# A four-layer block on one core: the last two of 39 expert blocks behind a condition, and regrouped activation tables

## The chip, the cores and the metric

The kernel runs on one core of a Trainium2 chip. Its five engines work side by side, each through its own instructions in order, and wait for one another by semaphores: TensorE (PE in the profile, with its weight loads as PEld), VectorE (DVE), ScalarE (ACT), GpSimd (POOL), and SyncE (SP), which here mostly issues transfers. The metric is the time of one execution on the device in microseconds (us); the median of several runs is compared. Everything is computed in 32-bit floats.

## The reference

x is 4 batches of 512 tokens with 512 channels. Four sublayers are added to it in turn. Each takes as input a gated value, a bidirectional decaying scan over the side input f, multiplied by a sigmoid of x:

```python
x = x + mamba2(gate0(x, f))        # 16 heads, inner width 1024, state 128
x = x + experts(gate1(x, f))       # 8 experts, each token goes to its best 2
x = x + attention(gate2(x, f))     # 16 causal heads of 128, keys in 4 groups
x = x + ffn(gate3(x, f))           # inner width 1408, silu(g) * u
```

The Mamba layer ends with a normalization and a projection, in which a weight per channel stands between the two:

```python
yg = yg * rsqrt(mean(yg * yg) + eps)
y = (yg * norm_w) @ out_proj_w.T
```

The expert layer:

```python
top_vals, top_idx = top_k(x @ gate_w.T + gate_b, 2)
routing = softmax(top_vals)
for e in range(8):
    h = x @ w1[e].T + b1[e]
    y = h[:, 0::2] * sigmoid(1.702 * h[:, 0::2]) * (h[:, 1::2] + 1)
    out += (y @ w2[e].T + b2[e]) * sum(routing * (top_idx == e))
```

## The kernel before, in words

Channels lie on the 128 partitions, tokens along the free axis. The program is written as one long unrolled stream, and a scheduler puts each engine's instructions in an order; `after(...)` pins what is written inside it behind the last instruction so far of the named engines.

**Gates.** `gate_pair` computes the part of a gate that doesn't depend on x, for two channel chunks at a time: scans on DVE, Exp and Ln on ACT. `make_gates` is a generator over the pairs; `pump` moves it on by one larger step, `nudge` by a small one. They are called between other work. `gated` loads such a gate, takes Tanh of x on ACT (`apply_gate`, L379 to L385) and multiplies on DVE.

**Activation tables.** ACT computes a function only with the table that holds it. `Tables` (`act`, L96 to L130) lets the kernel place the loads: `act.use(name)` puts one behind all activations that used the last, and `act(...)` an activation behind it. After `act.leave()` (L1400) tables are loaded wherever the compiler finds that one is missing. `LOG_EXP` holds Ln and Exp, `EXP` holds Exp and Tanh.

**Mamba stage** (L861 to L1412). Rows are the four batches, tiles are 128 tokens. The loop at L1298 interleaves, for each tile, the outputs of this tile (`decays`, `outputs`), the end of the tile before it (`squares`, `norm`, `turn`, `project`, `scale`, `add_x`), the start of the next, gate steps, and the routing of the batch before (`choose_experts`, with `logits` and `route`, a generator that is moved on by `next(routing)`). `turn` transposes y on PE and writes it times `norm_w` to yT: the first half by one DVE instruction (L1219), the second by four of ACT (L1227). `sums` forms cumulative sums by products with triangular matrices (L981); it copies the first, cs, out of PSUM (L991), transposes it on PE (L993), and copies that out again for a store (L995). `route` builds one-hot matrices ov and os on DVE (L571 to L574) and multiplies them on PE (L576).

**Expert stage.** Rows are gathered by expert into blocks of 128. However the tokens fall, 4096 rows fill at most 39 blocks (`NBLK`), since each of the 8 experts can leave one partly full. All 39 are computed; a block without tokens gathers a dummy row and its result goes nowhere. The first 17 (`NEARLY`) need only batches 0 to 2 and start within the Mamba stage. `order_blocks` gives each used block its place; of the last 22, those with tokens of batch 0 come first. `Experts.round` (L828) does, for block i: gather block i+3 (POOL), load weights if the expert in this slot changes (SP, a conditional transfer), the first half of the products (pg, pn), the transposes of block i-1, the last product of block i-2 (po), whose result POOL scatters to `rows_o`. Two rounds past the last block drain the pipeline.

The driver (L1476 to L1505) runs the rounds with one `pump` each until round 35, and from round 35 on adds batch 0's results to x (`load_results` by POOL, `add_results`: ACT, DVE, transposes pcb on PE, DVE). Then `early_h`, the first attention input, is gated from x[0], and two more rounds follow, beside which it can be computed.

**Attention** (L1509 to L1671). 64 heads: `queries` of the next head (pq), `scores` of this one (psc, mask and row maximum on DVE, Exp on ACT at L1592, division on DVE), `context` of the last (transposes ptp, copies pT, products pctx), and `dense` after each four. After each softmax row block a `nudge` moves the gates of layers 2 and 3. In the first group, at the second head of batch b, `combine(b + 1)` and the gate of batch b + 1 are written (L1656 to L1658). The feed-forward layer follows with its own loads.

Of the kernel before, what the change touches and what calls it, by code (L numbers as in the profile page):

```python
# [10 lines left out]
F32 = mybir.dt.float32  # L11
# [25 lines left out]
NROW = B * T * TOPK + 1  # L37

NEARLY = -(-((B - 1) * T * TOPK - E * (P - 1)) // P)

FIRST = (T * TOPK + E * (P - 1)) // P

# [38 lines left out]
def block_kernel(ctx: ExitStack, tc: tile.TileContext, a: dict, out: bass.AP):  # L81
# [363 lines left out]


    places = tmp.tile([P, NBLK], I32, tag="th", name="places")
    for lo, hi in ((0, FIRST), (FIRST, NBLK - NEARLY)):
        half = (hi - lo + 1) // 2
        nc.gpsimd.iota(places[:, lo : lo + 2 * half], pattern=[[1, half], [half, 2]], base=lo,  # L450
                       channel_multiplier=0)
# [55 lines left out]
    def route(lg, b, fine):  # L507
        n = NT * E
        bt_ = slice(b * NT, (b + 1) * NT)
        i1, i2, v1, v2 = is1[:, bt_], is2[:, bt_], g1[:, bt_], g2[:, bt_]  # L510
# [52 lines left out]
            nc.vector.tensor_copy(s_, ri)  # L563
            vq.append((q, s_))
        yield
        pt = ps_tp("ptok")
        over = lambda v: v.unsqueeze(2).to_broadcast([P, NT, P])
        lanes = lane.unsqueeze(1).to_broadcast([P, NT, P])
        for c, (q, s_) in enumerate(vq):
            ov = tmp.tile([P, NT, P], F32, tag="th", name="ov")  # L570
            nc.vector.tensor_tensor(ov, lanes, over(q), ALU.is_equal)  # L571
            nc.vector.tensor_tensor(ov, ov, over(res_id[c][:, bt_]), ALU.mult)
            os_ = tmp.tile([P, NT, P], F32, tag="th", name="os")
            nc.vector.tensor_tensor(os_, lanes, over(s_), ALU.is_equal)  # L574
            for t in range(NT):
                nc.tensor.matmul(  # L576
                    pt[:, :P], lhsT=ov[:, t, :], rhs=os_[:, t, :],
                    start=(t == 0 and c == 0), stop=(t == NT - 1 and c == 1),
                )
# [15 lines left out]
    def choose_experts(b, xb, parts, pool, fine=False, **kw):  # L595

        lg = rt.tile([P, NT, E], F32, tag="lg", name="lg", bufs=2)
        nt = NT // parts
        for i in range(parts):
            h = gated(1, b, xb, pool, slice(i * nt * P, (i + 1) * nt * P), **kw)  # L600
            if fine:
                yield
            logits(h, b, lg, i * nt, nt)
            yield
        yield from route(lg, b, fine)
# [6 lines left out]
    eb = rt.tile([1, NBLK], I32, name="eb")  # L612

    def order_blocks(lo, hi):

# [12 lines left out]
        if lo == 0:  # L628
            nc.tensor.matmul(pi[:, P : P + 1], lhsT=tri_lt, rhs=use, start=True, stop=True)
            nc.vector.tensor_copy(rank, pi[:, P : P + 1])  # L630
        else:

            two = rt.tile([P, 2], F32, tag="two", name="two")
            nc.vector.tensor_tensor(jk, sel, cnt[:, NT, :], ALU.mult)
            nc.vector.tensor_reduce(rank, jk, AX.X, ALU.add)
            nc.vector.tensor_scalar(two[:, 0:1], v_lo, rank, use, ALU.is_lt, ALU.mult)
            nc.vector.tensor_tensor(two[:, 1:2], use, two[:, 0:1], ALU.subtract)
            nc.tensor.matmul(pi[:, P : P + 2], lhsT=tri_lt, rhs=two, start=True, stop=True)
            nc.tensor.matmul(pi[:, P + 2 : P + 3], lhsT=ones, rhs=two[:, 0:1], start=True, stop=True)

            nc.vector.tensor_scalar(
                rank, pi[:, P + 1 : P + 2], pi[:, P + 2 : P + 3], two[:, 1:2], ALU.add, ALU.mult
            )
            nc.vector.scalar_tensor_tensor(
                rank, pi[:, P : P + 1], two[:, 0:1], rank, ALU.mult, ALU.add
            )
# [26 lines left out]
    class Experts:  # L673
# [48 lines left out]
        def know(self, n):  # L722

            self.known = n
            for i in range(self.i, min(n, self.i + self.LOOK)):
                self.fetch(i)
            if n == NBLK:
                self.weights(NEARLY)

        def fetch(self, i):  # L730
            if i >= self.known or i in self.hb:
# [96 lines left out]
        def round(self):  # L828
            i = self.i
            self.fetch(i + self.LOOK)  # L830
            if i < NBLK:
# [11 lines left out]
            if i >= 2:  # L843
                self.down(i - 2)
            self.second_weights(i - 2)
            if i < NBLK:
# [14 lines left out]
    with ExitStack() as ph:  # L861
# [63 lines left out]
            nc.sync.dma_start(out=wzt[:, k, :], in_=a["in_projT"][k * P : (k + 1) * P, :DI])  # L925
        nc.sync.dma_start(out=wot, in_=a["out_projT"].rearrange("(k p) m -> p k m", p=P))

        def time_steps(w):

            h = w.h  # L930
# [42 lines left out]
        def sums(w):  # L973
# [13 lines left out]
            dte = sm.tile([P, NT, NH], F32, tag="dte", name="dte", bufs=2)  # L987
            nc.vector.tensor_tensor(dte, dt, ex[:, 1], ALU.mult)

            cs = sm.tile([P, n], F32, tag="cs", name="cs", bufs=2)  # L990
            nc.vector.tensor_copy(cs, pp[:, :n])  # L991
            pcs = ps_tp("pcs")
            nc.tensor.transpose(pcs[:n, :P], cs, ident)  # L993
            csT = four[:n, 0:2, :].rearrange("p i t -> p (i t)")
            nc.vector.tensor_copy(csT, pcs[:n, :P])  # L995
            nc.sync.dma_start(out=cs_d[w.b], in_=csT)
            w.cs, w.ex, w.dte = cs, ex, dte

# [211 lines left out]
        def turn(u):  # L1210

            u.yT = sm.tile([P, NDI, P], F32, tag="yT", name="yT")
            for hh in range(2):
                pyt = ps_tp("pyt")
                for j in range(4):
                    js = slice(j * P, (j + 1) * P)
                    nc.tensor.transpose(pyt[:, js], u.y[hh][:, js], ident)
                if hh == 0:
                    nc.vector.tensor_tensor(  # L1219
                        u.yT[:, :4, :],  # L1220
                        pyt.rearrange("p (j t) -> p j t", t=P),
                        col("norm_w", 0, 4).unsqueeze(2).to_broadcast([P, 4, P]),
                        ALU.mult,
                    )
                else:
                    for j in range(4):
                        nc.scalar.mul(  # L1227
                            u.yT[:, 4 + j, :], pyt[:, j * P : (j + 1) * P], col("norm_w", 4 + j)
                        )

        def project(u):

# [65 lines left out]
        for b in range(B):  # L1298
# [6 lines left out]
            for t in range(NT):  # L1305
# [85 lines left out]
                pump(1, last_gates)  # L1391
                with after(*ENGINES):
                    next(routing, None)
                    if b == B - 1 and t == 1:
# [76 lines left out]
    with tc.tile_pool(name="moe_w2", bufs=1, reuse_waits="tile") as wm:  # L1471
# [4 lines left out]
        def more(limit):  # L1476
            while moe.i < min(limit, moe.known):
                moe.round()
                if moe.i < NBLK - NT:
                    with after(nc.vector):  # L1480
                        pump()

        more(moe.i + 1)
        next(routing)
# [26 lines left out]
    with att as ph:  # L1511
# [64 lines left out]
        def scores(u, i, qT):  # L1576

            prs = []
            for qi in range(NT):
# [12 lines left out]
                nc.scalar.activation(pr, psc[:, :n], AF.Exp, bias=nmax, accum_out=rsum)  # L1592
# [51 lines left out]
        def begin(n):  # L1644
# [4 lines left out]
                groups[g, b] = start_group(g, b, weights[g])  # L1649
            return groups[g, b], queries(groups[g, b], i)  # L1650

        groups = {}
        ready, held = begin(0), None
        for n, (g, b, i) in enumerate(heads_):
            u, qT = ready
            if g == 0 and i == 1 and b + 1 < B:  # L1656
                combine(b + 1)
                hs[b + 1] = gated(2, b + 1, x[b + 1], gp, tag="h", name=f"h2_{b + 1}")  # L1658
            if n + 1 < len(heads_):
                ready = begin(n + 1)  # L1660
            prs = scores(u, i, qT)
            if held is not None:
                old, done = held
# [5 lines left out]
        dense(held[0])  # L1669
        for _ in making:  # L1670
            pass  # L1671


    with ExitStack() as ph:
# [9 lines left out]
        for b in range(B):  # L1684
            h = gated(3, b, x[b], gp, tag="h", name=f"h3_{b}")
            hd = []
            for i in range(NFF):
# [12 lines left out]
                nc.scalar.activation(hi, pg, AF.Silu, scale=col("gate_s", i))  # L1700
# [86 lines left out]
```

## Time and profile before

| | |
|---|---|
| median of 3 runs | 2587.08 us (2586.99 to 2592.27) |
| the profiled execution's own time | 2591.44 us |
| its span, first to last instruction | 2589.7 us |
| mean granted TensorE clock | 0.978 |
| PE busy | 2446.0 us |
| DVE busy | 1409.8 us |
| ACT busy | 1032.3 us |
| POOL busy | 250.4 us |
| moved by DMA | 244.09 MB |
| activation table loads | 68, of 1283 ns each |

The profile is one execution; its span and what lies around it make up its time, and it need not be the median run. "Busy" is the time in which an engine had an instruction under way; an idle stretch is put down to what released the next instruction. A matrix product of 128x128 by 128x512 in 32-bit floats appears as two MATMUL instructions. PE is nearly always busy, so a microsecond counts where PE stands still or where PE has less to do.

### The profile page before, as it was taken

The page shows a single profiled execution, that of the slowest core. Times are in us where ns is not written, and L with a number is a line of the kernel's source. Part 1 is how long each engine was busy: PE and PEld are TensorE (multiplying, and loading weights), DVE is VectorE, ACT ScalarE, POOL GpSimd, SP SyncE. Part 2 cuts the span into 40 slices and gives each one's busy share as a digit, 9 for nine tenths or more (in the row PEclk, how much of TensorE's full clock was granted, in tenths as well). Part 3 has the DMA queues.
Part 4 walks back from the last instruction along what each step waited for, and adds up shares of the span by engine and source line. Part 5 has one row for each costly group of instructions (what it writes and reads, how often), then busy time and mean ns, then how long its engine had stood idle before and what let it go on. Part 6 is the DMA issues. An engine that isn't in the chain of part 4 may idle for free.

```text
span 2589.7 us, 24584 instructions
## 1 busy us (share of the span) xinstructions
PE 2446.0 (94%) x8204; PEld 1301.0 (50%) x8204; DVE 1409.8 (54%) x2786; ACT 1032.3 (40%) x2129; POOL 250.4 (10%) x301
## 2 busy tenths in 40 slices
PE   3889998999999999999989999999999999999999
PEld 1555555556544444445545555555555554444444
DVE  8789998997335555646686554556544441010010
ACT  4666756657222333325554444344443431000000
POOL 1031323313211111120000000000000000000000
PEclk9979998999899999999999999999999999999999
DMA  6222523324244697745231101110000012000000
GB/s 217 77 94 76 188 69 112 131 80 159 66 175 140 223 337 283 274 177 163 75 92 46 46 27 29 45 45 30 21 25 17 17 69 82 17 0 16 8 8 16
DMA packets 88510, 244.09 MB, mean 94 GB/s; under 512 B 9536, under 2 KB 19136, under 8 KB 79296
## 3 DMA queue, kind: packets, MB, share of 16 engines
q1 hardware_dynamic: 79200, 215.78, 24.3%
q0 software_dynamic: 6880, 22.55, 2.5%
q10 hardware_dynamic: 2304, 4.20, 0.4%
q8 instruction: 65, 1.06, 0.2%
q14 instruction: 61, 0.50, 0.1%
HBM read 284.82 MB, written 47.05 MB: 128 GB/s over the span
## 4 chain that ended last, share of the span: by engine, by line
PE 75%; DVE 16%; ACT 4%; DMA 3%; issue 1%; POOL 0%; SPq 0%; ACTq 0%; DVEq 0%
PE pd L1629 8%; PE pq L1565 7%; PE pfu L1696 6%; PE pfo L1706 6%; PE pfg L1691 6%; PE pctx L1614 5%; PE po L808 5%; PE pg L775 5%; PE pn L786 5%; PE psc L1582 3%; PE pc L1007 2%; PE po L1235 2%; PE pv L1551 2%; PE ptp L1605 2%; PE pz L1078 2%; PE pk L1543 2%
## 5 line engine op out<-in xcount | busy, mean ns | idle before, releaser
L1565 PE MATMUL pq<-h,wq 128*128 128x512 f32 x512 | 248.0, 600 | 10.9 <-ACT pr L1592 10.9
L1629 PE MATMUL pd<-cx,wd 128*128 128x512 f32 x512 | 222.9, 593 | 1.3 <-DVE xr L1637 1.3
L1007 PE MATMUL pc<-h,wxb 128*128 128x512 f32 x320 | 151.6, 629 | 46.1 <-DVE h L1275 39.0
L1700 ACT ACTIVATE hd<-pfg,cols 128x512 f32<-128x512 f32 x44 | 30.3, 688 | 380.8 <-PE pfg L1691 380.8
L1701 DVE SCALAR_TENSOR_TENSOR hd<-pfu,cols,hd 128x512 f32<-128x512 f32 x44 | 33.0, 751 | 269.1 <-PE pfu L1696 269.0
L1585 DVE TENSOR_TENSOR psc<-psc,mask 128x128 f32<-128x128 f32 x256 | 72.2, 288 | 192.9 <-PE psc L1582 192.9
L1592 ACT ACTIVATE pr<-psc,nmax 128x128 f32<-128x128 f32 (+3 forms) x256 | 135.5, 530 | 95.6 <-DVE nmax L1587 94.9
L1614 PE MATMUL pctx<-pT,v 128*128 128x512 f32 (+3 forms) x512 | 153.6, 443 | 8.5 <-ACT pT L1608 5.1
L1696 PE MATMUL pfu<-h,ffu 128*128 128x512 f32 x352 | 158.7, 592 | 0.8 <-DMA ffu<-in_upT 0.8
L1691 PE MATMUL pfg<-h,ffg 128*128 128x512 f32 x352 | 158.6, 592 | 0.0
L1582 PE MATMUL psc<-kT,qT 128*128 128x128 f32 (+3 forms) x512 | 153.1, 439 | 3.1 <-ACT qT L1573 1.6
L1629 PEld LDWEIGHTS pd<-cx,wd 128*128 128x128 f32 x512 | 95.9, 190 | 116.8 <-issue 110.0
L1706 PE MATMUL pfo<-hd,ffd 128*128 128x512 f32 x352 | 151.7, 592 | 0.0
L775 PE MATMUL pg<-w,hT 128*128 128x512 f32 x312 | 144.7, 606 | 4.3 <-DMA w<-in_w1x 4.3
L1614 PEld LDWEIGHTS pctx<-pT,v 128*128 128x128 f32 x512 | 93.4, 190 | 99.6 <-issue 35.9
L808 PE MATMUL po<-w,yT 128*128 128x512 f32 x312 | 142.3, 596 | 1.2 <-DMA w<-in_w2x 1.2
L786 PE MATMUL pn<-w,hT 128*128 128x512 f32 x312 | 140.7, 592 | 0.0
L1637 DVE TENSOR_TENSOR xr<-xr,pd 128x512 f32<-128x512 f32 x64 | 44.0, 687 | 169.3 <-PE pd L1629 169.3
L1587 DVE TENSOR_REDUCE nmax<-psc 128x1 f32<-128x128 f32 (+3 forms) x256 | 124.0, 486 | 2.6
L1007 PEld LDWEIGHTS pc<-h,wxb 128*128 128x128 f32 x320 | 62.6, 201 | 119.6 <-issue 73.8
L1565 PEld LDWEIGHTS pq<-h,wq 128*128 128x128 f32 x512 | 87.1, 192 | 69.4 <-issue 56.1
L1605 PEld LDWEIGHTS ptp<-ident,pr 128*128 128x128 f32 x640 | 77.8, 142 | 87.4 <-issue 38.4
(308 smaller groups left out, 4220.2 us busy)
## 6 DMA issues: line engine op xcount, KB each, us to landing
w<-in_w1x SPq DMA_DIRECT2D x80, 1024.0 KB
w<-in_w2x SPq DMA_DIRECT2D x40, 1024.0 KB
wb<-in_b1x SPq DMA_DIRECT2D x40, 512.0 KB
lm<-cs SPq DMA_DIRECT2D x32, 512.0 KB
kt<-in_fT SPq DMA_DIRECT2D x62, 256.0 KB
ek<-ek SPq DMA_DIRECT2D x62, 256.0 KB
ekv<-ekv SPq DMA_DIRECT2D x62, 256.0 KB
g<-num SPq DMA_DIRECT2D x30, 512.0 KB
```

What stands on the lines that cost most here:

```text
L775: nc.tensor.matmul(pg, lhsT=hT[:, k, :], rhs=self.w1[s][0][:, k, :], start=(k == 0), stop=(k == NC - 1))
L786: nc.tensor.matmul(pn, lhsT=hT[:, k, :], rhs=self.w1[s][1][:, k, :], start=(k == 0), stop=(k == NC - 1))
L808: nc.tensor.matmul(po, lhsT=yT[:, j, :], rhs=self.w2[s][:, j, :], start=(j == 0), stop=(j == NI - 1))
L1007: nc.tensor.matmul(pc, lhsT=wxb[:, k, m * P : (m + 1) * P], rhs=h[:, k, :], start=(k == 0), stop=(k == NC - 1),)
L1565: nc.tensor.matmul(pq, lhsT=u.wq[:, k, i * KVC : (i + 1) * KVC], rhs=u.h[:, k, :], start=(k == 0), stop=(k == NC - 1),)
L1582: nc.tensor.matmul(psc[:, :n], lhsT=qT[:, qi * P : n], rhs=u.kT[:, :n], start=True, stop=True)
L1592: nc.scalar.activation(pr, psc[:, :n], AF.Exp, bias=nmax, accum_out=rsum)
L1614: nc.tensor.matmul(pctx[:, kj * P :], lhsT=u.v[:, kj, :], rhs=pT[:, kj, kj * P :], start=(kj == 0), stop=(kj == NT - 1),)
L1629: nc.tensor.matmul(po, lhsT=u.wd[:, i, m * P : (m + 1) * P], rhs=u.ctxT[i], start=(i == 0), stop=(i == HPG - 1),)
L1691: nc.tensor.matmul(pg, lhsT=wg[:, k, cs], rhs=h[:, k, :], start=(k == 0), stop=(k == NC - 1))
L1696: nc.tensor.matmul(pu, lhsT=wu[:, k, cs], rhs=h[:, k, :], start=(k == 0), stop=(k == NC - 1))
L1706: nc.tensor.matmul(po, lhsT=wdn[:, i, m * P : (m + 1) * P], rhs=hd[i], start=(i == 0), stop=(i == NFF - 1),)
```

## The change

The number of blocks that are always computed becomes 37 (`ALWAYS`). `order_blocks` also counts the blocks in use behind the first 17 by a product with ones; all engines load that number into a register, and four rounds that compute the last two blocks stand in a part that is entered only if it is over 20. The drain of the first 37 takes the rounds in which the results of batch 0 are added, and `early_h` is written straight before the condition. Rounds in this stretch pump one gate step and two in turn.

```diff
+ALWAYS = NBLK - 2
...
-    for lo, hi in ((0, FIRST), (FIRST, NBLK - NEARLY)):
+    for lo, hi in ((0, FIRST), (FIRST, ALWAYS - NEARLY), (ALWAYS - NEARLY, NBLK - NEARLY)):
...
+            nc.tensor.matmul(pi[0:1, P + 3 : P + 4], lhsT=ones[:, 0:1], rhs=use, start=True, stop=True)
+            nc.vector.tensor_copy(in_use, pi[0:1, P + 3 : P + 4])
...
-                if moe.i < NBLK - NT:
+                if moe.i < ALWAYS - NT + 1:
                     with after(nc.vector):
-                        pump()
+                        pump(1 + moe.i % 2)
...
-        moe.know(NBLK)
+        moe.know(ALWAYS)
         more(NBLK - 8)
...
-        more(min(NEARLY + FIRST + 2, NBLK - NT - 1))
+        more(NEARLY + FIRST + 2)
...
         for t in range(NT):
-            more(moe.i + 1)
+            moe.round()
             with after(nc.tensor, nc.vector, nc.scalar):
                 add_results(0, t, results.pop(t))
...
-        assert moe.i == NBLK
+        assert moe.i == ALWAYS + 2
         early_h = gated(2, 0, x[0], wa, tag="wq", name="h2_0")
-        moe.round()
-        moe.round()
+        used = nc.values_load(in_use[0:1, 0:1], min_val=0, max_val=NBLK)
+        with tc.If(used > ALWAYS - NEARLY):
+            moe.i = ALWAYS
+            moe.know(NBLK)
+            for _ in range(4):
+                moe.round()
```

`Experts.round` and `know` are adapted to the two numbers. With it come changes elsewhere. In attention the softmax's Exp goes through `act` with the LOG_EXP table, the gate of the next batch moves one head later, between two table loads, and the feed-forward's silu goes through `act` too:

```diff
-                nc.scalar.activation(pr, psc[:, :n], AF.Exp, bias=nmax, accum_out=rsum)
+                act(pr, psc[:, :n], AF.Exp, bias=nmax, accum_out=rsum)
...
+        with after(nc.scalar):
+            act.use(act.LOG_EXP)
...
                 combine(b + 1)
-                hs[b + 1] = gated(2, b + 1, x[b + 1], gp, tag="h", name=f"h2_{b + 1}")
             if n + 1 < len(heads_):
                 ready = begin(n + 1)
+            if g == 0 and i == 2 and b + 1 < B:
+                act.use(act.EXP)
+                hs[b + 1] = gated(2, b + 1, x[b + 1], gp, tag="h", name=f"h2_{b + 1}")
+                act.use(act.LOG_EXP)
```

In the Mamba stage `norm_w` is multiplied once into the projection's weights, by POOL, so that `turn` only copies; the transposed cumulative sum is a product of its own; and `route` builds the first pair of one-hot matrices one step earlier, in h1's buffer:

```diff
+        for k in range(NDI):
+            nc.gpsimd.tensor_scalar(wot[:, k, :], wot[:, k, :], col("norm_w", k), None, ALU.mult)
...
+            nc.tensor.matmul(
+                pp[:n, 3 * n : 3 * n + P], lhsT=dA.rearrange("p t h -> p (t h)"), rhs=tri_le,
+                start=True, stop=True,
+            )
             cs = sm.tile([P, n], F32, tag="cs", name="cs", bufs=2)
             nc.vector.tensor_copy(cs, pp[:, :n])
-            pcs = ps_tp("pcs")
-            nc.tensor.transpose(pcs[:n, :P], cs, ident)
             csT = four[:n, 0:2, :].rearrange("p i t -> p (i t)")
-            nc.vector.tensor_copy(csT, pcs[:n, :P])
+            nc.vector.tensor_copy(csT, pp[:n, 3 * n : 3 * n + P])
...
-                if hh == 0:
-                    nc.vector.tensor_tensor(
-                        u.yT[:, :4, :],
-                        pyt.rearrange("p (j t) -> p j t", t=P),
-                        col("norm_w", 0, 4).unsqueeze(2).to_broadcast([P, 4, P]),
-                        ALU.mult,
-                    )
-                else:
-                    for j in range(4):
-                        nc.scalar.mul(
-                            u.yT[:, 4 + j, :], pyt[:, j * P : (j + 1) * P], col("norm_w", 4 + j)
-                        )
+                nc.scalar.copy(
+                    u.yT[:, hh * 4 : (hh + 1) * 4, :].rearrange("p j t -> p (j t)"), pyt
+                )
...
+            if fine and c == 0:
+                both = pool.tile([P, 2, NT, P], F32, **kw)
+                ov, os_ = both[:, 0], both[:, 1]
...
+            if fine and c == 0:
+                yield
```

For the last row one more `next(routing)` makes up for the added step.

More of the change, by code (lines that the diff above doesn't have):

```diff
@@ L505, in logits, with route @@
             nc.sync.dma_start(out=rows_h[lo : lo + P, :], in_=hr)
-    def route(lg, b, fine):
+    def route(lg, b, fine, pool, **kw):
         n = NT * E
@@ L565, in route @@
         yield
-        pt = ps_tp("ptok")
         over = lambda v: v.unsqueeze(2).to_broadcast([P, NT, P])
         lanes = lane.unsqueeze(1).to_broadcast([P, NT, P])
+        pt = None
         for c, (q, s_) in enumerate(vq):
-            ov = tmp.tile([P, NT, P], F32, tag="th", name="ov")
+            if fine and c == 0:
+                both = pool.tile([P, 2, NT, P], F32, **kw)
+                ov, os_ = both[:, 0], both[:, 1]
+            else:
+                ov = tmp.tile([P, NT, P], F32, tag="th", name="ov")
+                os_ = tmp.tile([P, NT, P], F32, tag="th", name="os")
             nc.vector.tensor_tensor(ov, lanes, over(q), ALU.is_equal)
             nc.vector.tensor_tensor(ov, ov, over(res_id[c][:, bt_]), ALU.mult)
-            os_ = tmp.tile([P, NT, P], F32, tag="th", name="os")
             nc.vector.tensor_tensor(os_, lanes, over(s_), ALU.is_equal)
+            if fine and c == 0:
+                yield
+            if pt is None:
+                pt = ps_tp("ptok")
             for t in range(NT):
@@ L604, in choose_experts @@
             yield
-        yield from route(lg, b, fine)
+        yield from route(lg, b, fine, pool, **kw)
     taken = rt.tile([P, 1], F32, name="taken")
@@ L611, in block_kernel @@
     idx_o = rt.tile([P, NBLK], I32, name="idx_o")
-    eb = rt.tile([1, NBLK], I32, name="eb")
+    eb = rt.tile([1, NBLK + 1], I32, name="eb")
+    in_use = eb[:, NBLK:]
     def order_blocks(lo, hi):
@@ L726, in know @@
                 self.fetch(i)
-            if n == NBLK:
-                self.weights(NEARLY)
+            if n > NEARLY:
+                self.weights(self.i if n == NBLK else NEARLY)
         def fetch(self, i):
@@ L830, in round @@
             self.fetch(i + self.LOOK)
-            if i < NBLK:
+            if i < self.known:
                 self.weights(i)
@@ L842, in round @@
                     self.yT[i - 1] = self.finish(self.y.pop(i - 1))
-            if i >= 2:
+            if i - 2 in self.yT:
                 self.down(i - 2)
             self.second_weights(i - 2)
-            if i < NBLK:
+            if i < self.known:
                 self.flip(i + 1)
@@ L1393, in block_kernel @@
                     next(routing, None)
-                    if b == B - 1 and t == 1:
+                    if b == B - 1 and t < 2:
                         next(routing)
@@ L1671, in block_kernel @@
             pass
+        act.use(act.SILU)
     with ExitStack() as ph:
@@ L1699, in block_kernel @@
                 hi = sm.tile([P, T], F32, tag="hd", name="hd", bufs=NFF + 2)
-                nc.scalar.activation(hi, pg, AF.Silu, scale=col("gate_s", i))
+                act(hi, pg, AF.Silu, scale=col("gate_s", i))
                 nc.vector.scalar_tensor_tensor(hi, pu, col("up_s", i), hi, ALU.mult, ALU.mult)
```

## The prediction

> **What bounds the kernel now.** I read the page first. TensorE (PE) is busy 94% of the span, and in the chain of work that ended last it holds three quarters:
>
> ```profile
> PE 75%; DVE 16%; ACT 4%; DMA 3%; issue 1%; POOL 0%; SPq 0%; ACTq 0%; DVEq 0%
> ```
>
> So time is won in two ways only: fewer PE instructions, or shorter PE idle stretches. Summed over the span, PE is idle 2589.7 - 2446.0 = 143.7 us; 41.8 us of it is the start (until 42 us), whose PE order the change leaves as it is. The busy time by stretch (us, then busy time and instruction count of PE, weight load, DVE, ACT, POOL; granted clock; DMA) shows where the rest lies:
>
> ```profile
> 160.00:600.00 440.00, 417.42 (x1686) 245.96 (x1686) 396.83 (x660) 292.81 (x568) 114.08 (x125) 0.95 0.31 102
> 860.00:1160.00 300.00, 293.98 (x841) 140.79 (x840) 164.91 (x211) 86.22 (x127) 55.79 (x56) 0.99 0.73 266
> 1160.00:2130.00 970.00, 932.36 (x3388) 517.27 (x3387) 543.49 (x1363) 446.88 (x1053) 2.79 (x4) 0.99 0.15 47
> ```
>
> In the Mamba stage (first row) PE idles 22.6 us of 440, with DVE at 90%: two engines are near their limit. In the expert stage PE idles 6.0 of 300, so it sets the pace. In attention it idles 37.6 of 970, while DVE and ACT are half free: there it is single waits that cost. The list of waits names the owners of what the change touches (total us, times, longest):
>
> ```profile
> PE pq L1565 <- ACT pr L1592: 10.9, 5, 2.5
> PE pp L1094 <- DVE yT L1219: 7.9, 3, 4.8
> ...
> PE ptok L576 <- DVE ov L572: 4.7, 4, 1.9
> ...
> PE pcs L993 <- DVE cs L991: 3.0, 3, 1.8
> ```
>
> **Part 1, the conditional blocks.** Is the part entered? I counted the reference's own top-2 choices on its inputs: 445, 1766, 393, 17, 483, 772, 163, 57 rows for the eight experts, or 4+14+4+1+4+7+2+1 = 37 blocks of 128. The test is "more than 20 in use behind the first 17"; 37 - 17 = 20, so it is not entered, by a margin of none in blocks but of 26 tokens in the expert nearest to one more (1766 against 14 x 128 = 1792). The trace agrees: its 244.09 MB fit 17 weight loads of 3.9 MB, which is what these counts give in the order of the blocks.
>
> What goes: two rounds. The end of the expert stage on PE (start, duration, line):
>
> ```profile
> 1149.28 3.60 PE L775 MATMUL pg<-w,hT 128*128 128x512 f32 x8
> 1152.71 0.60 PE L799 MATMUL pyt<-ident,u 128*128 128x128 f32 x4
> 1153.15 3.60 PE L786 MATMUL pn<-w,hT 128*128 128x512 f32 x8
> 1156.58 1.88 PE L808 MATMUL po<-w,yT 128*128 128x512 f32 x4
> 1159.01 0.63 PE L1460 MATMUL pcb<-ident,rr 128*128 128x128 f32 x4 [0.55 <-DVE rr L1455]
> 1159.47 0.60 PE L799 MATMUL pyt<-ident,u 128*128 128x128 f32 x4
> 1159.91 5.32 PE L808 MATMUL po<-w,yT 128*128 128x512 f32 x12
> 1165.06 1.88 PE L1543 MATMUL pk<-h,wkv 128*128 128x512 f32 x4
> ```
>
> There is no gap but 0.55 us. From start to start, pg and pn take 3.43 us each (1152.71 - 1149.28), po the same (4 MATMULs in 1.72), pyt and pfl 0.44 each: 3 x 3.43 + 2 x 0.44 = 11.17 us a block, **22.3 us** for two. All of it is on the path.
>
> What is late next: now the last po (5.15 us, 1159.91 to 1165.06) hides the gate of the first attention input: pcb, DVE add (0.69), ACT tanh (L121), DVE product (L383), then pk. In the new order the fourth pcb is PE's last instruction ahead of the branch, so that chain is bare. From pcb's start: 0.66 to the add (1159.01 to 1159.67), 0.69 add, about 0.3 handover, 0.6 tanh, 0.3, 0.66 product, 0.2 = 3.4 us, less the 0.5 that pcb itself runs: 2.9 us idle. Only the first of four products stands ahead of the branch on DVE; the branch's cost comes between it and the second, where pk's first chunk gives 0.86 us of cover. Further, the results for the fourth add are loaded only when the second's buffer is free. PE has pyt, po x4, pcb, po x2 between those two (about 6.5 us); in this trace POOL's issues lie 0.9 us apart and the two loads are followed by 1.5 us on ACT and DVE, so with some 3 us of transfer (estimate; a 256 KB gather lands in 5.8 us here by its row) it is about even: 0 to 2 us lost.
>
> The branch itself is not in this trace. From below: SP's register loads take 0.27 us (median of 39), so load, compare, wait for the engine's own last result and jump are not under 0.5 us. [...] The skipped text is short (49 instructions on PE, 15 on DVE, 12 on ACT as written), so I take the lower side, 0.8 us, and 0.2 of it is under pk's cover. [...]
>
> Seam: 2.9 + 0.6 + 1 - 0.55 (the gap that goes) = about 4 us, between 2.4 and 10. Part 1 is **-18.3**.
>
> **Part 2, activation tables and gates.** In attention each gate pair does Ln, which is outside the table of the softmax's Exp, and the table is swapped there and back, 11 times. On ACT:
>
> ```profile
> 1529.19 1.28 ACT L121 ACT_TABLE_LOAD   x1
> 1530.48 1.15 ACT L121 ACTIVATE rec<-rec,tiny 128x1024 f32<-128x1024 f32 x1
> 1531.65 1.28 ACT L1592 ACT_TABLE_LOAD   x1
> 1532.95 0.37 ACT L1592 ACTIVATE pr<-psc,nmax 128x128 f32<-128x128 f32 x1
> ```
>
> and on PE at that time:
>
> ```profile
> 1533.46 1.98 PE L1565 MATMUL pq<-h,wq 128*128 128x512 f32 x4 [2.50 <-ACT pr L1592]
> ```
>
> The pair of loads costs 2.57 us and PE waits 2.50: the wait is the swap. The same shape stands at 1292 (2.44), 1321 (1.41), 1604 (3.28), 1691 (2.48), 1839 (2.50), 1924 (2.66): 17.3 us with this one, of which I take back 16. [...] The trace has the 1283, but the next instruction starts at once (1530.48, 1532.95). 22 loads become 6 (order of the built program): 20.5 us of ACT by the row[...]
>
> The six that remain frame the tanh of the inputs for batches 1 to 3. They add 2.57 us each on ACT among softmax work that today needs no swap, and the gate now has one head's time (about 14 us) before pk needs it, not two: 0 to 3 us each, I take 1.3, so +4. The doubled pump on odd rounds moves three of 16 gate pairs into the expert stage (8 there now, 5 before): per pair 8 scans x 1.26 + 4.2 + 3.8 = 18 us of DVE, 54 us less in attention. That ends small waits (0.2 to 1 us) there: -2. In the expert stage DVE goes from 55% to about 80%; what it delays, u, has 6.9 us until pyt needs it (a pg and a po). I charge +1 for late weights. Sum of part 2: **-13**.
>
> **Part 3, the Mamba stage.** yT leaves DVE: 16 x 0.68 = 10.9 us of an engine at 90%; ACT trades 4 x 365 ns for 2 copies of 590 ns, 0.3 us less per tile. The waits on yT are 8.9 us (pp 7.9, po 1.0); ACT, at 67%, can be late too, so I take 5. The new product for cs^T skips the copy and transpose: of 3.0 us, 0.8 lies ahead of a wait for ACT that stays, so 2. The early ov and os: half of 6.4 us (ov 4.7, g 1.7), 3. POOL scales wot, 8 x 128x512, between 15 and 118 us where it is idle: at 0.73 us per 128x128 (L921) and 1.14 to 1.54 per 128x512, about 10 us, done long before its first use at 142. Should DVE be held up meanwhile, that costs 1 to 2 us; I charge 1. Sum **-9**, between -15 and +1.
>
> **Total.** -18.3 - 13 - 9 = -40 against this execution's 2591.44 (span 2589.7 and 1.7 around it). The median shown is 2587.08, 4.4 below that execution; taken off it: 2547, and I say **2548**.
>
> **Rivals.**
> (a) Only the blocks count: the rebuilt order makes new waits as large as those removed in Mamba and attention. For it: the scheduler reorders much of PE's Mamba part, and ACT stands in the path in both stages. Against: seven waits of one cause vanish. 2587 - 18 = **2569**, with a dear branch 2575.
> (b) More goes than I count: fewer stalls raise the granted clock in Mamba (0.95) and the gate-free softmax loses nearly all its 37 us of waits: -55, **2532**.
> (c) Slower: the doubled gates throttle the expert stage. SP issues in order, gate loads wait there for DVE to free kt and ekv, and the weights stand behind them; the DMA share there is already 73%, and late weights held PE 3.75 us once. 17 rounds run at the new rate; from 40 / 17 = 2.4 us lost per round on, all is given back; at 3 us the time is **2598**. Against: in this trace such waits sum to 5.5 us in 22 rounds.
> (d) The part is entered: the two blocks return (+22) unhidden, with gather (5.8) and weights bare, some 2587 to 2592. The counts exclude it but for other inputs.
>
> **Chances.** Forecast (2538 to 2560) 0.60, (a) 0.22, (b) 0.12, (c) 0.04, (d) 0.02. The range 2530 to 2570 takes in most of (a) and (b). Within 0.2% (5 us) is no change that this kernel's measurement can tell: 0.03; slower 0.04; faster 0.93.
>
> **What would show it.** 37 x 8 = 296 instructions each at pg, pn, po, not 312; 2 to 10 us of PE idle before the first pk, named after L383's product; seven table loads after the branch with the FFN's; PE's wait on pr under 3 us in attention; none on yT by DVE; PE idle in the expert stage still below 10 us. I am wrong if pg shows 312, if the seam is over 10 us, if weights hold PE in most rounds, or if attention's idle stays near 37 us.

## The result, and the profile after

The changed kernel took a median of 2560.95 us (2553.84 to 2565.35, 4 runs). The kernel before, on the same chip, took 2588.14 us (2586.99 to 2592.27, 4 runs). The ratio is 0.9898, with a 95% interval from 0.9880 to 0.9917; the medians differ by 27 us. The profiled execution took 2560.14 us, with a span of 2558.4 us. The median lies inside the stated range of 2530 to 2570 us, but 13 us above the forecast of 2548 and 1 us above the band of 2538 to 2560 that was given 0.60, on the side of rival (a). The interesting part is where these 13 us are, because the sum hides larger errors of opposite sign.

The page after, first the line of engine totals, then the chain of work that ended last:

```profile
PE 2420.2 (95%) x8146; PEld 1288.4 (50%) x8146; DVE 1402.9 (55%) x2771; ACT 1012.0 (40%) x2074; POOL 271.9 (11%) x306
...
PE 49%; DVE 4%; ACT 2%; DMA 0%; issue 0%; ACTq 0%; SPq 0%; DVEq 0%
```

PE's busy time fell by 25.8 us. The shares of the chain add up to only 55%, 1407 us: it can't be followed back over the condition, at about 1151 us, so this view no longer tells anything of the first half. The windows by stage do (us, then busy time and count of PE, weight load, DVE, ACT, POOL; granted clock; DMA share; GB/s):

```profile
160.00:600.00 440.00, 420.71 (x1752) 252.36 (x1751) 403.48 (x665) 300.84 (x565) 122.98 (x130) 0.97 0.32 107
860.00:1150.00 290.00, 277.18 (x784) 130.40 (x783) 187.56 (x233) 106.74 (x147) 52.28 (x52) 0.99 0.79 287
1160.00:2100.00 940.00, 922.15 (x3377) 516.45 (x3375) 507.73 (x1324) 399.12 (x999) 0.00 (x0) 1.00 0.13 43
```

PE's idle time in the Mamba window fell from 22.6 to 19.3 us and in attention from 37.6 to 17.9. In the expert window it rose from 6.0 of 300 us to 12.8 of 290, and that row does not even contain the worst of it. To see where time came from, cut each trace at three instructions of PE: the start of the last pot (the transposes that end Mamba), of the first pk (the keys, with which attention begins), and of the last pd (attention's last product).

| stage | before, us | after, us | difference | forecast |
|---|---|---|---|---|
| Mamba | 748.6 | 733.7 | -14.9 | -9 |
| experts, with the seam to attention | 416.5 | 424.8 | **+8.3** | -18.3 + 1 |
| attention | 965.3 | 940.2 | **-25.1** | -14 |
| the rest of the span | 459.4 | 459.7 | +0.3 | 0 |

The expert stage has two blocks fewer, 22.3 us of PE work (296 MATMULs at pg, not 312), and yet became longer. PE is busy 407.33 of the 416.5 us before and 394.74 of the 424.8 after, so its idle time here went from 9 to 30 us. PE's waits from 735 to 1165 us in the trace after (total us, times, longest) name what came in:

```profile
PE pg L788 <- DMA w<-in_w1x: 9.4, 4, 5.2
PE po L821 <- DMA w<-in_w2x: 7.0, 6, 2.0
PE pg L788 <- ACT hT L761: 4.2, 1, 4.2
PE pk L1556 <- DVEq L1514: 2.4, 1, 2.4
```

In the same window of the trace before, the waits for weights were

```profile
PE pg L775 <- DMA w<-in_w1x: 4.3, 2, 3.8
...
PE po L808 <- DMA w<-in_w2x: 1.2, 1, 1.2
```

and there was no wait on hT or at pk. (hT is the transposed input of pg, yT that of po.) Weights come late, and once ACT does. The timeline shows both kinds. SP's instructions, then DVE's and PE's, around the longest wait for weights (start, duration, line, tiles):

```profile
829.51 0.07 SPq L726 DMA_DIRECT2D wb<-in_b1x  x1
837.16 0.34 SPq L332 DMA_DIRECT2D g<-num  x1
837.91 0.34 SPq L721 DMA_DIRECT2D w<-in_w1x  x1
...
835.94 1.20 DVE L330 SCALAR_TENSOR_TENSOR num<-den,num 128x1024 f32<-128x1024 f32 x1
...
845.16 6.48 PE L788 MATMUL pg<-w,hT 128*128 128x512 f32 x8 [5.23 <-DMA w<-in_w1x]
```

SP issues nothing for 7.6 us. It stands at the store of a finished gate, which waits for DVE's last product; that ends at 837.14, the store goes out at 837.16, and the weights that stood behind it at 837.91. PE waits 5.23 us for them. The other kind, on ACT, and what PE made of it:

```profile
808.75 1.28 ACT L123 ACT_TABLE_LOAD   x1
810.04 1.15 ACT L123 ACTIVATE rec<-rec,tiny 128x1024 f32<-128x1024 f32 x1
811.21 1.28 ACT L123 ACT_TABLE_LOAD   x1
...
813.94 0.58 ACT L761 COPY hT<-pfl 128x512 f32<-128x512 f32 x1
...
814.57 6.43 PE L788 MATMUL pg<-w,hT 128*128 128x512 f32 x8 [4.18 <-ACT hT L761]
```

Two table loads of 1.28 us each, Ln and Exp of a gate stand ahead of the copy hT that PE needs. The swap that was taken out of attention is still made here, now eight times in place of five. Behind these two stops the pg takes 6.43 and 6.48 us where 3.60 is usual: the granted clock is then 0.51 (813.4 to 820.2 us) and 0.56 (845.2 to 851.6).

In attention no wait of the old kind is left; the largest row of PE's waits there is

```profile
PE pk L1556 <- ACT pr L127: 5.8, 3, 3.0
```

The 5.8 us are the three places at which the tanh of a gate and its two table loads stand on ACT ahead of the softmax for which pk waits.

### The profile page after: what moved, and what is told of

It is laid out like the page before. It is cut to its first block, busy times and chain, and to the rows that moved or that the text cites. A ratio compares the mean times of both kernels' runs of the same rounds, so it can differ in the third digit from the quotient of the medians.

```text
span 2558.4 us, 24369 instructions
## 1 busy us (share of the span) xinstructions
PE 2420.2 (95%) x8146; PEld 1288.4 (50%) x8146; DVE 1402.9 (55%) x2771; ACT 1012.0 (40%) x2074; POOL 271.9 (11%) x306
## 4 chain that ended last, share of the span: by engine, by line
PE 49%; DVE 4%; ACT 2%; DMA 0%; issue 0%; ACTq 0%; SPq 0%; DVEq 0%
PE pd L1642 8%; PE pq L1578 7%; PE pfu L1716 6%; PE pfo L1726 6%; PE pfg L1711 6%; PE pctx L1627 5%; PE psc L1595 4%; PE pv L1564 2%; PE ptp L1618 2%; PE pk L1556 2%; DVE nmax L1600 1%; DVE psc L1598 0%; ACT pr L127 0%; DVE num L258 0%; DVE den L258 0%; DVE den L264 0%
## 5 line engine op out<-in xcount | busy, mean ns | idle before, releaser
L821 PE MATMUL po<-w,yT 128*128 128x512 f32 x296 | 137.0, 603 | 7.6 <-DMA w<-in_w2x 7.0
L799 PE MATMUL pn<-w,hT 128*128 128x512 f32 x296 | 133.5, 593 | 0.0
L1586 ACT ACTIVATE qT<-pq 128x512 f32<-128x512 f32 x64 | 38.2, 596 | 235.8 <-PE pq L1578 221.4
```

Of the source, the lines that this page charges most:

```text
L821: nc.tensor.matmul(po, lhsT=yT[:, j, :], rhs=self.w2[s][:, j, :], start=(j == 0), stop=(j == NI - 1))
```

## The experiments

Times are medians; each ratio is to the kernel before, run on the same chip beside it (2585.0 to 2588.1 us), with its 95% interval. The table has every run, with the stages of its profiled execution cut as above. A stage's length in one execution scatters: without any edit to Mamba it was 748.6, 743.8 and 744.3 us.

| kernel | median | ratio | Mamba | experts | attention |
|---|---|---|---|---|---|
| before | 2588.1 | 1 | 748.6 | 416.5 | 965.3 |
| after | 2561.0 | 0.9898 (0.9880 to 0.9917) | 733.7 | 424.8 | 940.2 |
| Mamba part alone | 2578.2 | 0.9967 (0.9954 to 0.9979) | 735.0 | 417.1 | 963.6 |
| blocks alone | 2573.6 | 0.9948 (0.9933 to 0.9963) | 743.8 | 398.4 | 972.8 |
| attention tables alone | 2592.3 | 1.0023 (1.0014 to 1.0031) | 744.3 | 415.6 | 975.1 |
| after, no condition | 2564.1 | 0.9903 (0.9880 to 0.9927) | 736.4 | 425.8 | 943.4 |
| after, one pump | 2566.7 | 0.9924 (0.9907 to 0.9940) | 735.6 | 397.9 | 970.1 |
| after, one pump, early gate | 2557.8 | 0.9889 (0.9872 to 0.9907) | 738.3 | 398.9 | 959.2 |
| after, gates on POOL's queue | 2548.8 | 0.9853 (0.9837 to 0.9870) | 725.9 | 410.9 | 944.1 |
| after, only the store on POOL's queue | 2553.5 | 0.9876 (0.9853 to 0.9899) | 732.0 | 419.6 | 940.6 |
| after, no Ln | 2558.8 | 0.9891 (0.9872 to 0.9909) | 735.3 | 416.9 | 941.3 |
| after, gates on POOL's queue, no Ln | 2532.6 | 0.9803 (0.9786 to 0.9820) | 727.2 | 397.1 | 942.7 |
| after, a quarter pumped | 2546.3 | 0.9836 (0.9817 to 0.9856) | 733.4 | 404.8 | 946.9 |
| after, a quarter pumped, POOL's queue | 2538.7 | 0.9819 (0.9804 to 0.9835) | 736.4 | 397.1 | 945.1 |

The theory at the outset, called Q in the first expectations, was that the doubled gates are what spoils the expert stage: their transfers stand in SP's queue ahead of the weights. Rival B: the regrouped order of the blocks asks for weights at worse places, whatever the gates do. D: the condition is dear.

**One pump.**

```diff
-                        pump(1 + moe.i % 2)
+                        pump()
```

> The changed kernel, but one gate step per round in the expert stage as before. Theory Q (the doubled gate steps hold up the expert stage: ACT's reciprocal with its table swaps stands before hT, gate transfers stand before the weights on SP, and PE runs at half clock for a while after each long stop): PE's idle time between blocks 5 and 30 falls from some 24 us to under 8, no half-clock stretch there, three more gate pairs in attention cost 2 to 5 us; 2543 to 2551 us. Rival B (the regrouped blocks and the new order of their weights hold it up, not the gates): the waits stay, 2557 to 2565 us.

Measured: 2566.68 us, above the intervals of both theories. The stages show that Q was right about the expert stage and incomplete elsewhere. The expert stage takes 397.9 us, 26.9 less, and its waits for weights are as small as before:

```profile
PE pg L788 <- DMA w<-in_w1x: 3.8, 2, 3.5
...
PE po L821 <- DMA w<-in_w2x: 1.0, 1, 1.0
```

PE idles 12.2 us in it, 17.8 less than in the kernel after. The other 9.1 of the 26.9 us are no waits: the same products keep PE busy 385.65 us in place of 394.74. An estimate from the trace after puts part of it down to MATMULs at a low clock: there the eight behind the stops of 4.18, 5.23 and 2.02 us took 6.43, 6.48 and 5.40 us where 3.60 is usual, 7.5 us more in all; with one pump three waits for weights are left, of 4.8 us together. Attention became 29.9 us longer, by one stop. Around it, SP, DVE and PE:

```profile
1320.15 0.32 SPq L332 DMA_DIRECT2D g<-num  x1
...
1322.99 0.32 SPq L397 DMA_DIRECT2D h<-g  x1
...
1328.28 2.68 DVE L385 SCALAR_TENSOR_TENSOR h<-th,h 128x512 f32<-128x512 f32 x4 [6.90 <-DMA h<-g]
...
1332.05 5.16 PE L1556 MATMUL pk<-h,wkv 128*128 128x512 f32 x8 [27.31 <-ACT pr L127]
```

The label at the end names the softmax, but what all wait for is the gate: its last pair is stored at 1320.15 us, loaded back at 1322.99 and multiplied from 1328.28 on. ACT's last tanh, a table load and the softmax row of the label stand behind that, and then pk runs. This is the fourth batch's input (the expectations call it the second batch's). Its gate is the eighth of the pairs that attention's inputs need, two per batch. With the doubled pump seven pairs are stored by 1084 us and the eighth at 1184; with one pump five by 1083 and the eighth at 1320. So in this kernel, with the gate asked for one head later, the doubled pump buys about 30 us in attention and costs about 27 in the expert stage.

**No condition.** The register load, the condition and the last two blocks are left out:

```diff
-        used = nc.values_load(in_use[0:1, 0:1], min_val=0, max_val=NBLK)
-        with tc.If(used > ALWAYS - NEARLY):
-            moe.i = ALWAYS
-            moe.know(NBLK)
-            for _ in range(4):
-                moe.round()
```

> The changed kernel without the condition, the register loads and the last two blocks (which hold no tokens with these inputs). Theory Q: the branch itself costs under 1 us, the bare chain add-tanh-product stays: PE idles about 2 us before the first pk; 2557 to 2562 us. Rival D (the branch is dear[...]): 6 us or more go, 2550 to 2555 us.

Measured: 2564.13 us, above both intervals and not below the kernel after. The wait before the first pk is 2.17 us without the condition and 2.35 with it. D is out.

**The conditional blocks alone**, on the kernel before: the parts of the diff around `ALWAYS`, `in_use`, `know`, `round` and the condition, with one pump.

> The kernel before with the conditional blocks alone (one gate step per round, old Mamba stage, old tables). Theory Q: two rounds of 11.2 us go, the seam takes back 3 to 6 us, the expert stage's other waits stay as before (about 9 us); 2568 to 2572 us. Rival B: the expert stage loses some 15 us in blocks 9 to 14 here too; 2578 to 2586 us.

Measured: 2573.6 us, 13 us less, between Q's and B's. The expert stage is 398.4 us, 18.1 shorter, and rival B is refuted by it: the new order of the blocks costs no wait for weights. The missing 5 to 7 us are in attention, 972.8 us: PE waits 7.33 us from 1300 us on for the results of the fourth batch. Their loads leave SP's queue at 1299.56 us, straight behind the gate's loads that waited there, and then DVE still has that batch's gate to finish (stored at 1306).

**The gates' transfers on POOL's queue**, of the last two parts alone:

```diff
-            nc.sync.dma_start(out=kt[i], in_=...)
+            (nc.gpsimd if l >= 2 else nc.sync).dma_start(out=kt[i], in_=...)
```

and the same for ek, ekv and the store of g.

> The changed kernel, but the transfers of the gates of layers 2 and 3 (loads of k, ek, ekv and the store) are issued by POOL instead of SP, so that no weight load stands behind them. Theory Q: PE's waits for w fall from 16 us to under 6, the wait for hT (4.2 us) stays; 2546 to 2553 us. Rival B: the waits for weights stay, 2557 us or more; if the transfers themselves are the limit (bandwidth), the waits stay as well.

Measured: 2548.78 us, as Q said. PE's waits in the expert stage:

```profile
PE pg L788 <- ACT hT L761: 7.0, 3, 4.8
PE po L821 <- ACT yT L814: 4.2, 1, 4.2
```

The waits for weights went from 16.4 to 1.1 us (0.5 for w1, 0.6 for w2): SP's order is shown to be their cause. The same transfers are still made, at 255 GB/s over the expert stage for 248, so their rate is not what held the weights. What stays, 410.9 us against 398 with one pump, stands under ACT. In the kernel after, an issue waited for data with others behind it (7.6 us without an issue, until 837.16), and the choice of the issuing engine was worth 12 us (2561.0 to 2548.8).

**One pump with the early gate.** Is the stop of the first experiment made by the later place of the gate?

```diff
+                act.use(act.EXP)
+                hs[b + 1] = gated(2, b + 1, x[b + 1], gp, tag="h", name=f"h2_{b + 1}")
+                act.use(act.LOG_EXP)
             if n + 1 < len(heads_):
                 ready = begin(n + 1)
-            if g == 0 and i == 2 and b + 1 < B:
-                act.use(act.EXP)
-                hs[b + 1] = gated(2, b + 1, x[b + 1], gp, tag="h", name=f"h2_{b + 1}")
-                act.use(act.LOG_EXP)
```

> The kernel after with one pump in each round and with the gate of the next batch's input asked for one head earlier, at head 1 as in the kernel before (the two table loads round its tanh go with it). With one pump alone the expert stage won its 27 us back, but in attention the PE stood 27.3 us ahead of the second batch's pk, because the last gate pair of that batch was stored at 1320 us. Theory S (supply of gates: the doubled pump is needed in attention only because the gate is now asked for later and the PE runs out of other work): most of the stop goes, 2541 to 2553 us, faster than the kernel after by some 10 us. Rival L (the pair is late wherever it is asked for; only more pumping ahead of attention helps): a stop of 15 us or more stays, 2557 to 2570 us.

Measured: 2557.81 us, in L's interval, at its lower end, but without L's stop of 15 us or more. Attention is 959.2 us, 11 shorter than with the later gate; stops of 3.09 and 8.25 us stay at the same place (the pair is stored at 1303). Both are true in part: the later place adds to the stop, and the pair is late in either place.

**No Ln.** In the gates of the last two parts the Ln is a Relu of the same size, so the 16 table loads round it in the expert stage go; those gates then lack their reciprocal.

```diff
-        act(flat(r), flat(r), AF.Ln, bias=tiny[:, 0:1])
+        act(flat(r), flat(r), AF.Ln if l < 2 else AF.Relu, bias=tiny[:, 0:1])
```

> The kernel after, but in the gates of the last two parts the Ln is a Relu of the same size, so that the 16 table loads round it in the expert stage go (it leaves the reciprocal in those gates out). Theory T (the table swaps of the doubled gates hold the copies hT and yT, and with them the PE, beside what SP's queue costs): 3 to 11 us faster than the kernel after, 2550 to 2558 us. Rival (SP's queue alone is what the gates cost in the expert stage): within 2 us of the kernel after, 2559 to 2563 us.

Measured: 2558.75 us, between the two forecasts and inside the scatter of the kernel after: inconclusive in time. In its trace the longest wait on hT falls from 4.2 to 1.6 us, but those for weights stay (9.5 and 8.0). The same edit was therefore repeated with the weights freed, below.

**The Mamba part alone**, on the kernel before.

> The kernel before with the Mamba parts alone (yT copied by ACT with the norm weights multiplied into wot, cs transposed by a product, the early ov and os). By the prediction 9 us less, 2576 to 2580 us. By the profile after, whose Mamba stage ended 14.9 us earlier than before's, 13 to 16 us less, 2570 to 2574 us. If it was only the planner's new order: within 3 us of before.

Measured: 2578.2 us, 8.4 less: the forecast's 9. The 14.9 of the two profiled executions contain some 4.5 us by which before's was slow there, as the two kernels without an edit to Mamba show (743.8, 744.3).

**The attention tables alone**, on the kernel before: Exp through `act`, the later gate and its two loads, one pump.

> The kernel before with the attention's table hunks alone (Exp held to one table, the later gate with its two loads), one pump. By the prediction's sum for this part, -16 + 4: about 2575 us. By theory S the swaps' waits go (25 us or so) but the later gate puts a stop of 15 to 27 us ahead of the second batch's pk: 2577 to 2590 us, and the trace shows that stop. Rival: no stop, the full gain, 2558 to 2566 us.

Measured: 2592.34 us, 5.7 slower than before, just above the interval of theory S. PE's waits in attention begin with

```profile
PE pk L1543 <- ACT pr L125: 27.3, 3, 21.6
```

The stop of 21.6 us begins at 1341, behind the gate pair stored at 1350; it eats all that the tables save. On its own this part of the change is a loss.

**A quarter pumped, on POOL's queue.** If the extra pumping is only there to have the eighth pair in time, less will do:

```diff
-                        pump(1 + moe.i % 2)
+                        pump(1 + (moe.i % 4 == 3))
```

together with the gates' transfers on POOL's queue.

> The kernel after with the gates' transfers on POOL's queue and with two pumps in every fourth round instead of every second. Theory S (the extra pumping is there to have the last batch's gate ready before the PE asks for it at about 1330 us, and half of it is enough; each extra pump costs the expert stage 1 to 2 us): six gate pairs done in the expert stage, the eighth stored by about 1270 us, no stop of over 4 us in attention, expert stage 400 to 408 us (410.9 with all of them), 2539 to 2546 us, so below the kernel with the gates on POOL (2548.8). Rival (the eighth pair comes late again): a stop of 10 to 25 us, 2550 to 2565 us.

Measured: 2538.68 us, the shortest of the kernels that leave nothing out, 22 us below the kernel after. Six pairs are stored by 1063 us, the eighth at 1267. The expert stage takes 397.1 us, as little as with one pump, and PE's waits there are down to 2.3 us for weights and 1.3 us for hT.

**POOL's queue and no Ln**, with the doubled pump (it leaves the reciprocal of those gates out):

> The kernel after with the gates' transfers on POOL's queue and the Ln of the last two parts' gates a Relu (it leaves the reciprocal in those gates out). Theory T (what the doubled gates still cost the expert stage with their transfers off SP's queue, 410.9 us against 398, is ACT held by the table swaps): the waits of PE on hT and yT by ACT fall from 11.2 us to under 3, expert stage 398 to 403 us, 2537 to 2544 us. Rival (the rest is something else, DVE or the clock): 408 to 412 us of expert stage, 2546 to 2551 us.

Measured: 2532.55 us, even below theory T's interval, with an expert stage of 397.1 us. The wait of 4.2 us on yT is gone (0.3 us is left), and on hT there stay

```profile
PE pg L788 <- ACT hT L761: 2.7, 2, 2.1
```

So SP's queue and ACT's table swaps together account for the whole 27 us: 424.8, less 13.9 with the queue freed, less 13.8 more without the swaps (the shares hold for this order; the swaps taken away first were worth 7.9).

**Only the store on POOL's queue**:

```diff
-            nc.sync.dma_start(out=gts[l][b][:, c0 : c0 + 2, :], in_=g)
+            (nc.gpsimd if l >= 2 else nc.sync).dma_start(out=gts[l][b][:, c0 : c0 + 2, :], in_=g)
```

> The kernel after with only the store of each finished gate of the last two parts on POOL's queue; its loads stay in SP's. Theory St (the store, which waits in SP's queue for DVE's last product with the weights behind it, is what makes them late): most of the 12 us of the kernel with all gate transfers on POOL, 2549 to 2554 us, PE's waits on weights in the expert stage from 16.4 to under 5 us. Theory Ld (the loads, which wait for free buffers, do it): 2558 to 2562 us, waits on weights 12 us or more.

Measured: 2553.52 us. The time is in the interval of St, the waits are not: they fall from 16.4 to 8.0 us, not below 5. So about half of the weights' lateness is the store and the other half the loads in the same queue. Of the stage's 13.9 us the store alone gives 5.2 (419.6 us), since waits of 4.8 us on yT then come up.

**A quarter pumped, on SP's queue**: the one-line edit above alone.

> The kernel after with two pumps in every fourth round instead of every second, and the gates' transfers left on SP's queue: one number changed. Theory N (the loss in the expert stage goes with the number of gate pairs pulled into it; six instead of eight, five in the kernel before, cost about a third of the 27 us): expert stage 402 to 410 us, attention 941 to 947, 2542 to 2551 us. Rival (two pumps in one round upset SP's queue however seldom they come): expert stage 414 us or more, 2553 to 2562 us.

Measured: 2546.32 us, theory N. The expert stage is 404.8 us, attention 946.9. One number in the change was worth 15 us, without moving a queue.

## Why the prediction was right, and where it was not

**The blocks: right.** 22.3 us of PE work less 4 at the seam is 18.3; the expert stage with one pump shortened by 18.1 (blocks alone). The part is not entered: 296 MATMULs. At the seam PE waited 0.55, 1.54 and 2.35 us; less the 0.55 that was there before, that is 3.9 for the 4 forecast: 1.54 for the wait on results that was put at 0 to 2, and 2.35 for the bare chain and the condition that were put at 2.9 and 0.6. The condition itself can't be told from nothing (PE waited 2.17 us without it; PE's branch instruction took 0.24 us), so taking the lower side for it was right here; that it could be dear was not shown. POOL did wait there for its own scatter (1.69 us, until 1158.35), and SP's next transfer left at 1158.60 us, but PE needed nothing of theirs; POOL's wait stands behind its jump (1156.02). In time the blocks alone gave 13.2 us: by the profiles 7.5 went back to attention, through a wait that no term had.

**The Mamba part: right**, 8.4 for 9. PE waits for yT still, now by ACT (5.1 us in three waits, 8.9 before): 3.8 us came off where 5 were taken. The waits at ptok fell from 6.4 to 2.2 us, 4.2 for the 3 taken. That the sum agrees within 1 us is in part luck: waits that no term named also moved (pot for ACT's o from 1.2 to 4.0 us, pc for h from 7.1 to 4.0) and about cancel.

**The doubled pump in the expert stage: the step that failed.** It said of the doubled gates: "I charge +1 for late weights", because DVE, at 80%, still had 6.9 us to spare for u. DVE was not the problem; it is busy 65% of that window. The charge should have been 27 (424.8 against 397.9 with one pump), half of it SP's queue and half ACT. The sign set for it, PE idle below 10 us in the expert stage, failed with 30. Rival (c) named SP's half word for word, "gate loads wait there for DVE to free kt and ekv, and the weights stand behind them", and was given 0.04. What was weighed against it, 5.5 us of such waits in 22 rounds, were the waits of one pump a round, and the slack that one pump leaves does not tell what two cost. It had also left out two things: the store, and the low clock behind the two long stops (0.51 and 0.56). The second half, ACT, was in no step: the working took the swaps out of attention and did not ask where the gates that move take theirs.

**Attention: too small a gain, and for a reason not seen.** -16 + 4 - 2 were forecast, -25.1 came. The seven swap waits went, as said. The three tanh places cost 5.8 us for the 4, so that PE's waits on pr are 6.5 us and not under 3. But two terms were wrong. The tables with the later gate, -16 + 4, are +5 without the doubled pump (970.1 us with one pump, 965.3 before), because of the stop behind the eighth pair. And with the gate in that place "three of 16 gate pairs move, -2" should have been about -30: without them attention is 970.1 us, not 940.2. What the doubled pump would give with the gate in its old place was not run. The forecast treated the moved gates as DVE time to be saved and not as a due time. It looked at the later place of the gate, allowed 0 to 3 us for its tanh, and missed that a gate whose last pair isn't done yet must first finish that pair. The order of stores and loads of the gates in the trace before shows it: eighth store 1328.5 us, load 1331.4.

**The sum.** -18.3 - 9 were right; for the pump and tables together the forecast had -13, and the runs had +27 and -25, that is +2. The difference of 15 covers the 13 us by which the forecast was low. It is small by luck: the three terms were off by +26 (the pump in the expert stage), -28 (the pump in attention) and +17 (tables and later gate).

## What to carry to other kernels

- Before moving work from one stage to another, list every queue that it brings along, with what waits in each: here DVE had room, and the loss came from SP's queue, where the weights stood behind a gate's store (no issue for 7.6 us), and from ACT's table swaps (two loads of 1.28 us ahead of the copy hT).
- Work with a due time is moved by exactly as much as the due time needs. Half of the extra pumping gave three quarters of its gain in attention (946.9 us, between 970.1 and 940.2) for a quarter of its loss in the expert stage (404.8, between 397.9 and 424.8).
- A part of a change can be a loss alone (tables, +5.7 us) while the stage it is in gets shorter in company (attention, 25.1 us); what it is worth there is another measurement. Undoing a part can hide its cost behind another stage's stop, so read the stages and not only the time.

## What was not expected of the hardware

Two stops of PE cost more than their length. After those of 4.18 and 5.23 us the next eight MATMULs took 6.43 and 6.48 us for 3.60, at a granted clock of 0.51 and 0.56: 2.8 and 2.9 us more. Behind shorter stops in the same trace the clock was not always low:

```profile
877.38 5.40 PE L821 MATMUL po<-w,yT 128*128 128x512 f32 x8 [2.02 <-DMA w<-in_w2x]
...
1011.97 3.67 PE L788 MATMUL pg<-w,hT 128*128 128x512 f32 x8 [2.59 <-DMA w<-in_w1x]
```

The shorter stop was followed by a clock of 0.67 (877.4 to 882.6 us), the longer by 1.00 (1012 to 1015.5). So the length of the last stop alone does not tell what follows. At the seam two stops of 1.54 and 2.35 us, with 0.63 us of transposes between them, were followed by a pk of 5.14 us (granted clock 0.71, 1158.5 to 1163.5 us) where 3.70 is usual; without the condition the stops were 1.54 and 2.17 us, and pk took 6.35.

A table swap took no more than its load in the expert stage either: the Ln starts at 810.04, 0.01 us after the end of the load of 1.28 us that began at 808.75, and the Exp at 812.50, 0.01 us after the end of the one that began at 811.21.
